# A graph network on one core: the sort's mask transfers issued from GpSimd, three GpSimd steps moved to VectorE and ScalarE, and the sort written ahead of the next pair's neighbours

## The chip, the core and the metric

The kernel runs on one core of one Trainium2 chip. A core has TensorE (PE, matrix products), VectorE (DVE), ScalarE (ACT), GpSimd (POOL) and SyncE (SP), each with its own instruction queue, executed in order, and 16 DMA engines that all queues share. PEld is PE's loading of weights. SP, ACT and POOL can issue DMAs. The time is the device time of one execution in microseconds (us): 5809.48 us is the median of three runs (5806.7 to 5821.54).

## The reference

The input is 16 graphs of 1024 nodes with 64 features `x`, a symmetric adjacency matrix `adj` (zeros and ones, ones on the diagonal) and a node mask. Four layers follow one another, each adding its result to `x`, and each starting from `h = max(layernorm(x), 0)`.

Layer 0 first thins the graph. Of each node with more than ten neighbours, every `skip`-th neighbour is removed, in both directions. Then, for each node and feature, three quantiles over the remaining neighbours are taken and mixed:

```python
skip = jnp.where(nb > T, (nb + K - 1) // K, 1)
rem = neigh & (sk > 1) & (rank % sk == sk - 1) & mask[:, :, None]
rem = rem | jnp.swapaxes(rem, 1, 2)
adj_d = jnp.where(rem, 0.0, adj_)
...
s = jnp.sort(vals, axis=2)        # the neighbours' values of each feature
for tau, w in zip((0.25, 0.5, 0.75), (0.25, 0.5, 0.25)):
    agg = agg + w * (v_lo + frac * (v_hi - v_lo))
```

A small two-layer network follows. Layer 1 is a gated recurrent update with messages summed through `adj`, layer 2 a small network on sums through `adj`, and layer 3 an attention whose scores come from `adj` and the features, with a softmax over the first node index.

## The kernel before

The kernel works on pairs of graphs, eight in all. Instead of sorting the neighbours of every node, it sorts all 1024 nodes once per feature and finds each quantile by counting.

- **`sort_begin`, `sort_pair` (L752 to L881)**: the sort of one pair, with the 128 combinations of graph and feature on the 128 partitions and the 1024 nodes along the row. A bitonic network of 55 steps runs on DVE. Each forward step writes a mask of which elements were swapped (L791 or L793), their maxima (L794) and minima (L795). Four steps make a group; the group's masks, 512 KB, lie in one of two buffers `swapped` and are stored to DRAM (`m_d`, L808). After the last step the kernel walks back through the network: it loads the groups in reverse (L821) and carries rank codes to the places that the elements came from (L826 to L839). L842 to L870 build tables of the sorted values, and L873 to L881 transpose the codes and store them (`y_d`).
- **`neighbours` (L884 to L983)**: for each graph, eight tiles of `adj` are loaded (`a`, L898), turned into zeros and ones (L899), cleared on the diagonal (L900, on POOL), and summed along the row (L904). PE transposes each tile (L910), ACT copies it out (L912) and stores it (`a_d`, L913) for layers 1 to 3. Four tiles form a half; then small steps (L919 to L929) give each node's step, ACT marks the removed neighbours (L933 to L935), PE combines the marks of both directions (L954) and ACT writes the thinned matrix `ndT` (L960). The buffers `ni`, `rem` and `cum` exist once.
- **`weights`, `select` (L986 to L1247)**: comparisons of rank codes (L1000, on DVE), then counting by matrix products and picking of the quantiles.
- **`compact`, `extras` (L1252 to L1399)**: nodes that fall outside the tables' range are collected and treated apart. A gather issued by POOL (L1296) fetches their rows.
- **`layers` (L1415 to L1622)**: the rest of layer 0 and layers 1 to 3 of one graph. Every pass over `adj` loads eight tiles (`adj_block`, L1495). L1521 copies the mask and L1530 two halves of `hT`, both on POOL.

The loop over pairs (L1656) runs, for pair `pr`: weights, selection and compaction of both graphs; extras; layers of both graphs; and then, for the next pair, `prepare` (the neighbours of its two graphs) and `sort_pair`; at the end `sort_begin` for the pair after that. All of this is written as straight code. A scheduler arranges it: among the instructions that are ready on an engine in its model of time, the one that was written first goes first. So the place in the program is a priority, and each queue's order, SP's and POOL's among them, is fixed when the kernel is built. The first pair's sort is marked as high priority and stands in front of its neighbours. The pool that holds the neighbours' working tiles (`ni`, `rem`, `cum`, `a`) is closed before the one with the next pair's weights is opened, so the weights can be given the same memory, and then wait for the neighbours' last reads.

The order in question:

```python
if pr + 1 < pairs:
    made = prepare(pr + 1, nb, nbp)
    sort_pair(pr + 1, cur, sop)
```

Of the kernel before, what the change touches and what calls it, by code (L numbers as in the profile page):

```python
# [42 lines left out]
def gnn_stack(ctx, tc, x, adj, nodemask, w, out):  # L43
# [736 lines left out]
    def sort_pair(pr, cur, sop):  # L780

        nxt = row4()
        groups = range(0, len(steps), GROUP)
        for k0 in groups:
            swapped = next(swaps)
            for k, (size, j) in enumerate(steps[k0 : k0 + GROUP]):
                of = cut(size, j)
                lo, hi = halves(cur, size, j, of)
                to_lo, to_hi = halves(nxt, size, j, of)
                if size == N:  # L790
                    nc.vector.tensor_tensor(side(swapped[:, k, :], size, j), *halves(cur, size, j)[::-1], op=ALU.is_gt)  # L791
                else:
                    nc.vector.tensor_tensor(side(swapped[:, k, :], size, j, of), hi, lo, op=ALU.is_gt)  # L793
                nc.vector.tensor_tensor(to_lo, lo, hi, op=ALU.max)  # L794
                nc.vector.tensor_tensor(to_hi, lo, hi, op=ALU.min)  # L795
                if odd_even(size, j):
                    ends_ = slice(None, None, size // j - 1)
                    nc.vector.tensor_copy(inner(nxt, size, j)[:, :, ends_], inner(cur, size, j)[:, :, ends_])
                cur, nxt = nxt, cur
                if size < N and size in CUT and j == 2 * CUT[size][2]:  # L800
                    rest_ = so.tile([P, 1], F32, name="rest_", bufs=2)
                    nc.vector.tensor_reduce(
                        rest_, cur.rearrange("p (x w) -> p x w", w=CUT[size][0])[..., CUT[size][1] :],
                        axis=AX.XY, op=ALU.max,
                    )
                    nc.vector.tensor_max(past, past, rest_)
            n = len(steps[k0 : k0 + GROUP])
            nc.sync.dma_start(m_d[k0 // GROUP, :, :n], swapped[:, :n])  # L808
        srt = row4()
        for g in range(8):  # L810
            nc.scalar.copy(
                srt.rearrange("p (b a g l) -> p g l a b", a=2, b=2, g=8)[:, g],
                cur.rearrange("p (l r a b) -> p r l a b", r=8, a=2, b=2)[:, 4 * (g & 1) + (g & 2) + (g >> 2)],
            )
        code = so.tile([P, N], U16, name="code")
        nc.sync.dma_start(code, c0_d)
        xo = so.tile([P, N // 2], U16, name="xo")
        for k0 in reversed(groups):
            swapped = next(swaps)
            n = len(steps[k0 : k0 + GROUP])  # L820
            nc.sync.dma_start(swapped[:, :n], m_d[k0 // GROUP, :, :n])  # L821
            for k, (size, j) in reversed(list(enumerate(steps[k0 : k0 + GROUP]))):
                of = cut(size, j) if size < N else None
                lo, hi = halves(code, size, j, of)
                d = side(xo, size, j, of)
                nc.vector.tensor_tensor(d, lo, hi, op=ALU.bitwise_xor)  # L826
                if of is None and not odd_even(size, j):
                    nc.vector.tensor_mul(xo, xo, swapped[:, k, :])
                else:
                    nc.vector.tensor_mul(d, d, side(swapped[:, k, :], size, j, of))  # L830
                if odd_even(size, j):
                    pairs_ = between(code, d, size, j)
                else:
                    pairs_ = None if j == size // 2 and size > 32 else both_sides(code, xo, j, of)
                if pairs_ is None:
                    nc.vector.tensor_tensor(lo, lo, d, op=ALU.bitwise_xor)
                    nc.vector.tensor_tensor(hi, hi, d, op=ALU.bitwise_xor)
                else:
                    nc.vector.tensor_tensor(pairs_[0], *pairs_, op=ALU.bitwise_xor)  # L839


        nc.vector.tensor_max(past, past, srt[:, 2 * WL * (NH - 1) : 2 * WL * (NH - 1) + 1])  # L842
        used = 2 * WL * NH

        def differences(step):
            fl = row4()[:, :used]
            nc.scalar.mul(fl[:, :step], srt[:, :step], SCALE)
            nc.vector.tensor_sub(fl[:, step:], srt[:, step:used], srt[:, : used - step])
            nc.scalar.mul(fl[:, step:], fl[:, step:], SCALE)
            return fl  # L850

        def parts(to, src):
            nc.scalar.copy(to[0], src)
            nc.vector.tensor_sub(to[1], src, to[0])

        dif = differences(2 * WL).rearrange("p (a b c) -> p a b c", b=2, c=WL)
        parts([ttab[:, :, k, :, :WL] for k in range(2)], dif)
        nc.sync.dma_start(t_d[pr * P : (pr + 1) * P], ttab.rearrange("p a b c d -> p a (b c d)"))
        dif = differences(WL).rearrange("p (w c) -> p w c", c=WL)
        ends = so.tile([P, WL], F32, name="ends")  # L860
        at = 0
        for k in STATS:
            w0, w1 = WIN[k]
            n = w1 - w0
            parts([wtab[:, at + 1 : at + n, e, :WL] for e in range(2)], dif[:, w0 + 1 : w1])
            nc.vector.tensor_add(ends, srt[:, WL * w0 : WL * (w0 + 1)], srt[:, WL * (w1 - 1) : WL * w1])
            nc.vector.tensor_scalar_mul(ends, ends, SCALE)
            parts([wtab[:, at, e, :WL] for e in range(2)], ends)
            at += n
        nc.sync.dma_start(w_d[pr * P : (pr + 1) * P], wtab.rearrange("p w a l -> p w (a l)"))  # L870

        cf = row4()
        nc.scalar.mul(cf, code, -4.0)  # L873
        cn = row4().bitcast(F16)[:, :N].rearrange("p (t k) -> p t k", k=P)
        for q in range(0, NT, 4):
            pc = sop.tile([P, 4, P], F32, name="ps")
            for t in range(4):
                nc.tensor.transpose(pc[:, t, :], cf[:, (q + t) * P : (q + t + 1) * P], ident)
            nc.scalar.copy(cn[:, q : q + 4, :], pc)
        for b in range(2):  # L880
            nc.sync.dma_start(y_d[pr * 2 + b], cn[:, :, b * C : (b + 1) * C])  # L881


    def neighbours(b, ndT, row10, qb, qz, nb, nbp):  # L884
# [9 lines left out]
        for t0 in range(0, NT, HT):  # L894
            cum = nb.tile([P, HT, N], F16, name="cum")
            for t in range(t0, t0 + HT):
                a = nb.tile([P, N], F32, name="a", bufs=2)
                nc.sync.dma_start(a, adj[b, t * P : (t + 1) * P, :])  # L898
                nc.vector.tensor_single_scalar(ni[:, t, :], a, 0.0, op=ALU.is_gt, saturate=False)  # L899
                nc.gpsimd.tensor_mul(  # L900
                    ni[:, t, t * P : (t + 1) * P], ni[:, t, t * P : (t + 1) * P], offdiag, saturate=False
                )

                nc.vector.tensor_tensor_scan(  # L904
                    cum[:, t - t0, :], ni[:, t, :], wide[:, t, pad - 1 : pad - 1 + N], 0.0, op0=ALU.add, op1=ALU.add
                )
                for q in range(0, NT, 4):
                    pt = nbp.tile([P, 4, P], F32, name="pk")
                    for k in range(4):
                        nc.tensor.transpose(pt[:, k, :], a[:, (q + k) * P : (q + k + 1) * P], ident)  # L910
                    at = nb.tile([P, 4, P], F32, name="at", bufs=3)
                    nc.scalar.copy(at, pt)  # L912
                    nc.scalar.dma_start(  # L913
                        a_d[b % 4, q : q + 4, :, t * P : (t + 1) * P].rearrange("j p n -> p j n"), at
                    )
# [499 lines left out]
    def layers(b, side_, agg, front, ly, lb, h0, xb, held=None):  # L1415
# [24 lines left out]
        def own(v):  # L1440
            return v.rearrange("p (t f) c -> p t f c", f=2)
# [76 lines left out]
            )  # L1518
        x1 = nd("xs", 2)
        mask = ly.tile([P, NT, 1], F32, name="mask")  # L1520
        nc.gpsimd.tensor_copy(own(mask), by_half(maskf[:, b * NT : (b + 1) * NT].rearrange("p (t o) -> p t o", o=1)))  # L1521
        nc.vector.tensor_mul(x1, by_node(py), mask.to_broadcast([P, NT, C]))
        nc.vector.tensor_add(x1, x1, xb)

# [2 lines left out]
        hT = transposed(h1, "hT")  # L1527
        both_ = ly.tile([P, 2, HALF], F32, name="two")
        for f in range(2):
            nc.gpsimd.tensor_copy(both_[f * C : (f + 1) * C, f, :], hT[f * C : (f + 1) * C])  # L1530
        mT = packed("mT")
        nc.scalar.activation(mT, dense_p([(l1w1_d, hT)]), AF.Relu, bias=l1b1_t, scale=1.0)
        m2 = big()
# [122 lines left out]
    for pr in range(pairs):  # L1656
# [18 lines left out]
        with ExitStack() as beside:  # L1675
# [14 lines left out]
            with (  # L1690
# [9 lines left out]
                for i, (ly, lb) in enumerate(((ly0, lb0), (ly1, lb1))):  # L1700
                    layers(pr * 2 + i, (pr * 2 + i) % 4, aggs[i], ly0, ly, lb, *heads[i], held[i])
                if pr + 1 < pairs:
                    made = prepare(pr + 1, nb, nbp)
                    sort_pair(pr + 1, cur, sop)
                if pr + 2 < pairs:
                    cur = sort_begin(pr + 2, sop)
    lasting.close()
# [46 lines left out]
```

## Time and profile before

| what | value |
|---|---|
| median of three runs | 5809.48 us (5806.7 to 5821.54) |
| profiled execution | 5811.5 us, span 5809.6 us |
| PE busy | 4320.3 us (74%) |
| DVE busy | 5034.4 us (87%) |
| ACT busy | 3811.5 us (66%) |
| POOL busy | 257.3 us (4%), 308 instructions |
| DMA moved | 551.49 MB, mean 95 GB/s |
| mask stores and loads of the sort (L808, L821) | 112 each, issued by SP |
| L900 on POOL | 128 instructions, 89.6 us |
| L1530 on POOL | 32 instructions, 24.4 us |
| L1521 on POOL | 16 instructions, 3.1 us |

A row of the profile names an engine, a source line, an operation and the tiles that it writes and reads (written, arrow, read), with its count and times. "Idle before" is the time that the engine stood still just before such an instruction, and the releaser is what ended it. The chain of waits follows the work that ended last back through whatever released it. A queue's name with a small q (SPq, POOLq) means the instruction queue of that engine, which issues DMAs. The granted clock is TensorE's, as a share of full speed. Busy shares are means over stages with different limits, so most of what follows is read from a single stage.

### The profile page before, as it was taken

How to read it: one execution, taken by the hardware profiler on the slowest of the kernel's cores; microseconds unless marked ns; L12 is line 12 of the kernel's file. 1: busy time of each engine (PE TensorE's matmuls, PEld its weight loads, DVE VectorE, ACT ScalarE, POOL GpSimd, SP SyncE). 2: the span in 40 equal slices, each digit the busy share in tenths (PEclk: the TensorE clock that was granted, in tenths of full speed). 3: DMA queues.
4: the chain of work that ended last, by engine and by line, in shares of the span. 5: the costliest groups of instructions: out<-in, count | busy, mean ns of one | idle time of the engine just before them, and what ended most of it. 6: DMA issues, size and time to landing. Idle time of an engine off the chain costs nothing.

```text
span 5809.6 us, 114773 instructions
## 1 busy us (share of the span) xinstructions
PE 4320.3 (74%) x45010; PEld 2712.1 (47%) x45010; DVE 5034.4 (87%) x13519; ACT 3811.5 (66%) x5753; POOL 257.3 (4%) x308
## 2 busy tenths in 40 slices
PE   1488686896768958788677886688866887768966
PEld 1355443554435544455434554355543554435542
DVE  9999878998799987998889988899888998887765
ACT  1586657775676856768567675766657866568735
POOL 3000000000000000000100001000000000000000
PEclk5699787997889968899788997889977998889977
DMA  4401363014621046210571105611255112630030
GB/s 129 126 28 40 97 228 103 26 37 125 222 80 35 28 136 221 73 32 27 161 228 45 40 30 176 210 37 37 64 190 169 33 40 83 214 115 9 19 100 5
DMA packets 523657, 551.49 MB, mean 95 GB/s; under 512 B 264065, under 2 KB 413825, under 8 KB 523105
## 3 DMA queue, kind: packets, MB, share of 16 engines
q1 hardware_dynamic: 380704, 459.65, 25.3%
q10 hardware_dynamic: 140064, 81.84, 4.6%
q8 instruction: 355, 5.82, 0.4%
q0 software_dynamic: 2336, 2.57, 0.2%
q14 instruction: 198, 1.61, 0.1%
HBM read 360.17 MB, written 183.76 MB: 94 GB/s over the span
## 4 chain that ended last, share of the span: by engine, by line
DVE 37%; PE 32%; ACT 16%; DMA 11%; issue 3%; POOL 0%; SPq 0%; ACTq 0%; DVEq 0%; POOLq 0%
PE comb L1122 10%; ACT sign L1177 5%; DVE y L1193 5%; PE cand L1222 4%; PE comb L1311 4%; DVE cand L1230 3%; PE bank L1502 3%; DMA a<-in_adj_dram 2%; DVE cum L904 2%; ACT y L1130 2%; DMA adjT<-a_d 2%; DVE wt L1000 2%; DMA a_d<-at 2%; PE pk L954 2%; DVE code L839 2%
## 5 line engine op out<-in xcount | busy, mean ns | idle before, releaser
L1122 PE MATMUL comb<-wt,ndT 128*128 128x512 fp8e5 x6144 | 1445.0, 388 | 143.3 <-ACT sign L1177 112.6
L1130 ACT ACTIVATE y<-comb,qb 128x512 int16<-128x512 f32 x1152 | 744.9, 710 | 526.1 <-PE comb L1122 526.1
L1122 PEld LDWEIGHTS <-ndT 128*128 128x128 fp8e5 x6144 | 592.5, 99 | 862.8 <-issue 235.1
L1177 ACT ACTIVATE sign<-comb,lower 128x1024 fp8e5<-128x1024 int16 (+1 forms) x640 | 694.6, 1085 | 0.0
L1177 ACT ACTIVATE sign<-comb,half 128x1024 fp8e5<-128x1024 int16 (+1 forms) x640 | 689.2, 1077 | 0.0
L1193 DVE TENSOR_TENSOR y<-y 128x512 uint16<-128x512 uint16 (+5 forms) x896 | 669.5, 788 | 10.8 <-PE comb L1175 10.0
L1222 PE MATMUL cand<-vtab,sign 128*128 128x48 f16 (+1 forms) x18432 | 661.4, 191 | 17.4 <-DVE agg L1099 10.1
L1222 PEld LDWEIGHTS <-sign 128*128 128x128 fp8e5 x18432 | 636.6, 96 | 76.9 <-issue 23.6
L1230 DVE COPY_PREDICATED cand<-w_f,cand 128x256 f32<-128x256 uint16 (+1 forms) x1536 | 529.1, 377 | 75.9 <-PE cand L1222 73.6
L1175 PE MATMUL comb<-ident_b,y 128*128 128x128 bf16 x4608 | 307.2, 218 | 102.9 <-ACT sign L1177 70.6
L954 PE MATMUL pk<-ident_b,ni 128*128 128x128 bf16 x1024 | 234.9, 251 | 160.2 <-ACT at L912 90.3
L1175 PEld LDWEIGHTS <-y 128*128 128x128 bf16 x4608 | 284.8, 97 | 128.1 <-issue 127.8
L954 PE MATMUL pk<-minus_b,rem 128*128 128x128 bf16 x1024 | 235.9, 256 | 145.2 <-ACT rem L935 145.2
L912 ACT COPY at<-pk 128x512 f32<-128x512 f32 x256 | 146.3, 583 | 287.8 <-PE pk L910 150.1
L1000 DVE TENSOR_SCALAR wt<-node 128x2048 uint8<-128x2048 f16 x224 | 261.6, 1219 | 53.1 <-PE comb L1311 52.6
L904 DVE TENSOR_TENSOR_SCAN cum<-ni 128x1024 f16<-128x1024 fp8e5 x128 | 292.7, 2291 | 16.4 <-POOL ni L900 16.4
L910 PE MATMUL pk<-ident,a 128*128 128x128 f32 x1024 | 186.2, 325 | 134.1 <-DMA a<-in_adj_dram 90.8
L1502 PE MATMUL bank<-adjT,nd 128*64 128x512 f32 x896 | 252.1, 631 | 32.2 <-DMA adjT<-a_d 31.9
L794 DVE TENSOR_TENSOR s<-s 128x384 f32<-128x384 f32 (+4 forms) x440 | 264.9, 602 | 0.0
L1188 DVE TENSOR_SCALAR y<-y 128x4608 int16<-128x4608 int16 x128 | 173.4, 1354 | 104.1 <-ACT y L1130 104.1
L795 DVE TENSOR_TENSOR s<-s 128x384 f32<-128x384 f32 (+4 forms) x440 | 262.9, 597 | 0.0
L1502 PE MATMUL bank<-att,hs 128*64 128x512 f32 x512 | 192.7, 868 | 79.3 <-ACT hs L1612 78.6
(382 smaller groups left out, 8383.2 us busy)
## 6 DMA issues: line engine op xcount, KB each, us to landing
adjT<-a_d SPq DMA_DIRECT2D x336, 512.0 KB
a<-in_adj_dram SPq DMA_DIRECT2D x128, 512.0 KB
a_d<-at ACTq DMA_DIRECT2D x256, 256.0 KB
m_d<-swapped SPq DMA_DIRECT2D x104, 512.0 KB
swapped<-m_d SPq DMA_DIRECT2D x104, 512.0 KB
n_d<-nat SPq DMA_DIRECT2D x128, 128.0 KB
x_d<-xr SPq DMA_DIRECT2D x112, 128.0 KB
comb_x<-x_d ACTq DMA_DIRECT2D x24, 512.0 KB
```

Of the source, the lines that this page charges most:

```text
L794: nc.vector.tensor_tensor(to_lo, lo, hi, op=ALU.max)
L904: nc.vector.tensor_tensor_scan(cum[:, t - t0, :], ni[:, t, :], wide[:, t, pad - 1 : pad - 1 + N], 0.0, op0=ALU.add, op1=ALU.add)
L954: nc.tensor.matmul(pk[:, n % 4, :], lhs, rhs, start=(n % 4 == 0 and m == 0), stop=(m == len(terms) - 1 and last),)
L1000: nc.vector.tensor_scalar(wt[g][:, :, k : k + 4, :].bitcast(U8), node, 4.0 * (25 + CODE * (8 * g + k)), 4.0 * 26, op0=ALU.add, op1=ALU.min,)
L1122: nc.tensor.matmul(pw, ndT[:, j, t * P : (t + 1) * P], wt[1 + g8][:, j].rearrange("p w c -> p (w c)"), start=(j == 0), stop=(j == NT - 1),)
L1130: nc.scalar.activation(y[:, 0, chunks, at : at + 8 * d_].rearrange("p q (w d) -> p q w d", d=d_), pw.rearrange("p (w q d) -> p q w d", w=8 ...
L1175: nc.tensor.transpose(pt[:, q - q0, :], y[:, 0, q, :].bitcast(BF16), ident_b)
L1177: nc.scalar.activation(signs[tl][s][:, q0:q1, :], pt.bitcast(I16), AF.Sign, bias=before[s], scale=-1.0, saturate=False,)
L1193: nc.vector.tensor_tensor(v[:, :, :, :n], v[:, :, :, :n], v[:, :, :, n : 2 * n], op=ALU.max)
L1222: nc.tensor.matmul(cand[:, e, at : at + 12 * d_].rearrange("p (d l) -> p d l", l=12), signs[tl][sec][:, chunk, :], tab[:, q, :, half_ * 12 ...
L1230: nc.vector.copy_predicated(v[:, :, :, dst : dst + k], mk.to_broadcast([P, 2, C // 2, k]), v[:, :, :, frm : frm + k])
L1502: nc.tensor.matmul(po[to : to + C, :], lhs, rhs[:, f * HALF : (f + 1) * HALF], start=(j == 0), stop=(j == NT - 1))
```

## The change

The masks of the sort are stored and loaded through POOL's queue instead of SP's. Three elementwise steps leave POOL: the clearing of the diagonal and the copy of the mask go to DVE, the copy of `hT` goes to ACT. POOL keeps the memsets (L746, L891, L1334), a small copy (L968), the gather (L1296) and the loading of constants. In the loop, `sort_pair` for the next pair is written ahead of `prepare`, so it takes precedence over the neighbours wherever both are ready.

```diff
-            nc.sync.dma_start(m_d[k0 // GROUP, :, :n], swapped[:, :n])
+            nc.gpsimd.dma_start(m_d[k0 // GROUP, :, :n], swapped[:, :n])
...
-            nc.sync.dma_start(swapped[:, :n], m_d[k0 // GROUP, :, :n])
+            nc.gpsimd.dma_start(swapped[:, :n], m_d[k0 // GROUP, :, :n])
...
-                nc.gpsimd.tensor_mul(
+                nc.vector.tensor_mul(
                     ni[:, t, t * P : (t + 1) * P], ni[:, t, t * P : (t + 1) * P], offdiag, saturate=False
                 )
...
-        nc.gpsimd.tensor_copy(own(mask), by_half(maskf[:, b * NT : (b + 1) * NT].rearrange("p (t o) -> p t o", o=1)))
+        nc.vector.tensor_copy(own(mask), by_half(maskf[:, b * NT : (b + 1) * NT].rearrange("p (t o) -> p t o", o=1)))
...
-            nc.gpsimd.tensor_copy(both_[f * C : (f + 1) * C, f, :], hT[f * C : (f + 1) * C])
+            nc.scalar.copy(both_[f * C : (f + 1) * C, f, :], hT[f * C : (f + 1) * C])
...
                 if pr + 1 < pairs:
+                    sort_pair(pr + 1, cur, sop)
                     made = prepare(pr + 1, nb, nbp)
-                    sort_pair(pr + 1, cur, sop)
```

## The prediction

> **What bounds the kernel now.** The page comes first: which engine is full, and what the chain of waits that ended last is made of.
>
> ```profile
> PE 4320.3 (74%) x45010; PEld 2712.1 (47%) x45010; DVE 5034.4 (87%) x13519; ACT 3811.5 (66%) x5753; POOL 257.3 (4%) x308
> DVE 37%; PE 32%; ACT 16%; DMA 11%; issue 3%; POOL 0%; SPq 0%; ACTq 0%; DVEq 0%; POOLq 0%
> ```
>
> DVE is the fullest engine, but 13% of it is idle, and the chain changes engine often. The order of the starts shows a period: the weights (L1000) of pairs 1 to 7 begin at about 973, 1679, 2389, 3093, 3795, 4499 and 5199 us, every 700 to 710 us. A period is some 370 us of selection and compaction, and a side stage of about 316 us in which extras, layers, the next pair's neighbours and the next pair's sort share the engines. Next the busy time of each engine in stretches of one side stage (1365 to 1681):
>
> ```profile
> 1474.00:1510.00 36.00, 33.76 (x284) 20.50 (x284) 31.88 (x100) 17.66 (x32) 4.52 (x7) 0.95 0.61 213
> 1510.00:1556.00 46.00, 37.27 (x154) 15.64 (x155) 25.74 (x81) 25.70 (x37) 1.97 (x4) 0.96 0.89 310
> 1556.00:1653.00 97.00, 64.34 (x298) 29.11 (x296) 89.67 (x244) 74.95 (x100) 1.18 (x2) 0.77 0.54 163
> 1653.00:1669.00 16.00, 8.10 (x156) 6.79 (x152) 15.18 (x49) 9.18 (x15) 0.00 (x0) 0.90 0.41 99
> 1669.00:1681.00 12.00, 2.34 (x9) 1.57 (x10) 5.90 (x37) 3.64 (x6) 0.00 (x0) 0.50 0.22 33
> ```
>
> The columns are PE, PEld, DVE, ACT, POOL, clock, DMA share, GB/s. DVE is idle for 20.3 of 46 us from 1510 to 1556, and the last 12 us are nearly empty on every engine. SP's queue says why the sort stops in the first hole:
>
> ```profile
> 1533.46 14.07 SPq L1495 DMA_DIRECT2D adjT<-a_d  x8
> 1547.62 0.44 SPq L898 DMA_DIRECT2D a<-in_adj_dram  x1
> 1548.10 0.90 SPq L821 DMA_DIRECT2D swapped<-m_d  x2
> ```
>
> Two loads of the sort's masks leave back to back at 1548.10, though DVE had used up both buffers by 1509: they stood behind adjacency loads that wait for PE. The same hole is in every side stage. The chain shows the second hole:
>
> ```profile
> 1548.10 7.78 DMA swapped<-m_d
> ...
> 1668.00 0.64 DVE code L839
> 1668.66 1.07 ACT s L873
> ...
> 1673.32 2.93 DMA y_d<-s
> 1676.31 2.68 DMA node<-y_d
> 1680.98 13.73 DVE wt L1000 x12
> ```
>
> The sort's last step ends at 1668.6; its result crosses ACT, PE and DRAM twice before the weights start 12.3 us later. The neighbours' last large ACT step ends beside it, and layers ended at 1653:
>
> ```profile
> 1662.22 0.99 ACT L960 ACTIVATE ndT<-pk 128x512 fp8e5<-128x512 f32 x2 [0.25 <-PE pk L954]
> ```
>
> **The change part by part.** The profiled execution took 5811.5 us (span 5809.6, 1.9 around it), 2.0 above the median shown, 5809.48; the sum is made against it.
>
> *Mask transfers (L808, L821) from SP to POOL.* 112 stores and 112 loads, 28 per sort. SP's issue takes 0.32 us. POOL's plain DMAs at the start take 0.48 to 1.09 each and land after 1.5 to 3.0 us, but they are small (at most 32 KB); the sort's loads land in 3.97 and 7.78 us on the chain. So POOL adds between 0.16 and 0.77 us to a load. A group of four backward steps is about 4 x (0.42 + 0.42 + 0.69) = 6.1 us of DVE and the loads are one group ahead, which covers it; uncovered, 112 x 0.77 = 86 us is the upper end. I take 0.
> The Trainium skill, "SBUF — State Buffer", section "SBUF: two separate sides", speaks against this: descriptors of a GpSimd DMA cannot be written while DVE runs a two-port instruction, and a DMA of 620 ns took 3100. By that page an estimate would be 112 x 2.5 = 280 us if all loads lay open; no run here shows it, and the sort's own steps have two inputs, which the page excepts from that trap.
> What does SP gain? The hole, 20.3 us of idle DVE per side stage, is open to the sort. It isn't free: that stretch moves 310 GB/s at a DMA share of 0.89, and four loads more (2.1 MB) take 6.8 us of it. [...]
> New order on POOL: a store waits for DVE's compares (on SP the longest such wait is 16.1 us), and behind it stand the row gather (L1296), for which PE waits, the memsets (L891, L1334) and L968. A gather held for 16 us in all 16 batches would cost 256 us. I take 0: its index also comes from DVE, and later in DVE's order than a store put ahead of it.
>
> *Sort traced ahead of neighbours.* The sort then wins DVE whenever both are ready. Of its backward steps 45 us (L826, L828, L830, L836, L837, L839) lie after 1556; the hole has room for 20, and the scans and tests of the neighbours (L904, L899), 24 us of DVE from 1400 to 1556, now give way. So it should end between 1560 and 1600 instead of 1669, and its 12.3 us tail comes under other work. The end passes to the neighbours. They are four halves in a row (one buffer of L904's scans), each DVE, then ACT and PE: first scans at 1369, 1430, 1494, 1563. The best guide is the first stage, where the sort already has high priority: there halves start at 53, 115, 174 and 207 and end by 252, 199 us against 294 here, though the ten small steps of one half (L919 to L929) took from 80 to 102 between sort steps. So layers and loads, more than the sort, set the pace of the neighbours. If they still end at 1663, the weights follow 4.7 us later (from the issue of node's load to L1000), at 1668: 13 us saved. If they end with layers at 1653, 23 are saved, and 26 if node is loaded ahead: the upper end. If they slip by 13, nothing is saved; by 26, as much as the spread small steps held one half up in the first stage (its scans end at 78, its next ACT step starts at 103), 13 are lost: the lower end. I take a slip of 5, nearer to none, because their second and third halves lie under the sort and the last one doesn't: 8 us saved, 7 x 8 = -56.
>
> *L900 to DVE.* 128 products of 128x128; nearest rows 0.18 (L1201, 128x64), 0.22 (L1369, 128x128 uint16) and 0.29 (L1553, f32). 128 x 0.22 = 28 us, less the 16.4 that L904 waited for POOL: +12, of which some 10 where DVE is full. Ends: 0 and +21.
> *L1521 to DVE*: 16 x 0.16 = 2.6 us, early in a batch's layers while PE works: 0, or +3 uncovered.
> *L1530 to ACT*: 32 copies; nearest row 0.58 (L1315, 64x512): 19 us. They stand between hT and mT on ACT, where PE's product takes 1.06 us: 2 x 0.58 - 1.06 = 0.1 per batch, +2; +19 if another order leaves them open.
>
> *What POOL stops doing.*
>
> ```profile
> L900 POOL TENSOR_TENSOR ni<-ni,offdiag x128: 406/647/2326, 51.7 to 5129.5; 128x128 fp8e5<-128x128 fp8e5 x128
> L1296 POOL DMA_INDIRECT rows<-n_d,who x16: 952/1026/6518, 446.2 to 5549.1; - x16
> ```
>
> The first gather of pairs 1 to 7 takes 6.5 us and lands after 8.9; the second takes 0.97. Before the slow ones POOL ran products and copies, before the fast ones one small copy. If the mixture is the reason, 7 x 4 = 28 us go; but pair 0's first gather, behind products alone, took 1.3. Between 0 and -28 I take -14.
>
> Sum: -56 + 10 + 2 - 14, and +2 for the first stage, where 16 products less POOL's waits meet a full DVE: -56. 5811.5 - 56 = 5755.5, or 5754 on the scale of the median.
>
> **The rivals.** *Slower: the neighbours become the tail.* For it: with the sort first, ACT is idle early and the neighbours' ACT work (L933 to L960) falls into 1556 to 1653, where ACT is busy for 75 of 97 us with layers ahead of it. Against: the first stage's pace. It decides from a slip of 13 us on; with 26, the -56 turns into 7 x 13 = +91: 5754 + 56 + 91 = 5901.
> *Everything is gained*: SP also serves adjacency loads sooner, layers lose a competitor on DVE after 1556, and the neighbours end with layers. 7 x 24 (between 23 and 26) = 168 instead of 56, and the whole 28 of the gather: 5754 - 112 - 14 = 5628. Against: layers already come first.
> *No effect*: the sort was hidden, the neighbours slip by 11 to 13 us, and 0 to 14 us are left, the gather's -14 and the small costs of +14 cancel: 5796 to 5810, and DVE's new idle time stands at the end of the side stage.
> *POOL's queue is slow*: loads late by 0.77 us and the 6.8 us of shared DMA on the path in seven stages: 5754 + 86 + 48 = 5888. Against: loads are a group ahead.
>
> **How the numbers follow.** The likeliest has 0.47 (its own range 5690 to 5790), everything gained 0.12, no effect 0.09, neighbours as tail 0.24, slow queue 0.08. About 0.3%, 17 us, is what a measurement of this kernel can tell from no change; so faster 0.59, same 0.09, slower 0.32. The range, 5635 to 5890, holds all but 'everything gained' and the far end of 'the neighbours as tail'.
>
> **What would show it.** Right: no hole in DVE after the first third of layers; mask loads leave POOL right after the step that frees their buffer; the sort's last step well before layers end; the weights following the neighbours' last ACT step by 5 us; a period of about 695 to 700. Wrong: DVE waiting for masks, PE for the gather; L960 running 15 us or more past layers; the first gather still at 6.5 us. What would upset it all is a different order of layers or selection, since every order here follows from the trace order.

## The result, and the profile after

The changed kernel takes 6102.52 us (median of four runs, 6100.36 to 6124.92) beside 5810.12 us for the kernel before on the same chip: a ratio of 1.0502, 95% interval 1.0486 to 1.0518. The forecast was 5754. The profiled execution took 6101.26 us, with a span of 6099.5 and a granted clock of 0.815 (0.850 before). The lower clock goes with the order (0.826 with the order alone changed, 0.852 with the old order put back, both below), and the layers end no later at it: 671 us after the weights on average over five periods, 677 before.

The page of the changed kernel, its first line and its chain of waits:

```profile
PE 4416.2 (72%) x45010; PEld 2788.8 (46%) x45010; DVE 5090.4 (83%) x13663; ACT 3821.9 (63%) x5783; POOL 231.9 (4%) x356
DVE 37%; PE 35%; ACT 15%; DMA 8%; issue 3%; SPq 1%; ACTq 0%; DVEq 0%; POOLq 0%
```

DVE has 56 us more to do, of which L900 accounts for 128 x 0.28 = 36 us, and yet its share fell from 87% to 83%: the 290 us more are waiting, not work. The weights (L1000) of pairs 0 to 7 start at 275, 1030, 1775, 2522, 3267, 4014, 4762 and 5488 us. By the same count the kernel before has them at 275, 975, 1681, 2391, 3095, 3797, 4501 and 5200. The period is 745 to 748 us where it was 702 to 710, the first is 755 instead of 700, the last 726 instead of 699, and the seven differences add up to 288 us, so all of the loss lies in the seven side stages.

The same side stage as in the prediction (the period that starts at 1030), as busy time of each engine in five stretches of the changed kernel; columns as before, PE, PEld, DVE, ACT, POOL, clock, DMA share, GB/s:

```profile
1437.00:1497.00 60.00, 19.79 (x388) 18.36 (x387) 58.70 (x186) 15.38 (x15) 1.61 (x3) 0.50 0.26 84
1505.00:1560.00 55.00, 43.98 (x182) 24.37 (x183) 43.27 (x128) 28.59 (x41) 2.69 (x5) 0.66 0.60 198
1560.00:1616.00 56.00, 44.39 (x185) 18.87 (x186) 46.47 (x156) 26.38 (x42) 1.07 (x2) 0.88 0.77 262
1616.00:1701.00 85.00, 58.01 (x383) 28.33 (x382) 63.00 (x191) 70.23 (x97) 0.69 (x1) 0.80 0.52 152
1701.00:1775.00 74.00, 29.76 (x299) 23.96 (x297) 70.00 (x150) 41.28 (x56) 3.75 (x7) 0.65 0.38 127
```

Two things are new. In the first 60 us DVE is full while PE and ACT have little to do. And the last 74 us, after the layers have ended at about 1701, have no counterpart before, where layers ended 28 us ahead of the weights. VectorE is not idle there: of its 70 us, 54 are forward steps (L793 to L802) of the sort of the pair after next, of which 30 of 55 have run by the next weights and none had before. They are written later than the neighbours and fill what these leave.

The first stretch, in VectorE's own order (start, duration, line, tiles):

```profile
1435.45 0.68 DVE L899 TENSOR_SCALAR ni<-a 128x1024 fp8e5<-128x1024 f32 x1
...
1436.66 0.28 DVE L900 TENSOR_TENSOR ni<-ni,offdiag 128x128 fp8e5<-128x128 fp8e5 x1
1436.86 1.08 DVE L1362 TENSOR_SCALAR y_x<-y_x 128x3584 int16<-128x3584 int16 x1
...
1496.83 2.28 DVE L904 TENSOR_TENSOR_SCAN cum<-ni 128x1024 f16<-128x1024 fp8e5 x1
...
1501.23 0.16 DVE L919 TENSOR_TENSOR sk<-cum,ni 128x4 f32<-128x4 f16 x1
```

The fourth tile of the neighbours' first half is ready for its scan at 1436.9 and is scanned 60 us later. Adding up the instructions in between by line, 60 are the sort's (some 22 us) and 125 belong to the extras (some 37 us). Before, this half's last scan and its ten small steps ran at 1391.9 to 1396.2, just ahead of the extras' first DVE instruction at 1398.9. With the sort in front, the half misses that place, and then falls behind the extras too, which were written earlier still. ScalarE gets its work only now:

```profile
1508.23 1.15 ACT L933 ACTIVATE sq<-cum,sk 128x1024 f32<-128x1024 f16 x1 [25.29 <-DVE sk L927]
```

The halves form a chain: one `cum` buffer, and `ni` and `rem` are shared by the two graphs. Counted from the start of the weights, the small steps of the four halves stand at 470, 559, 676 and 711 us (period of 1775) against 420, 477, 568 and 640 before (period of 1681), so they are late by 50, 82, 108 and 71 us. The second graph can be seen to wait for the first: the memset of its `ni` (L891) stands at 647 us (period of 1030), where PE's last products on the first graph's `ni` (L954) end, and both stood at 516 to 517 before. The neighbours' last large ACT step (L960) ends on average at 737 instead of 687 over five periods, and layers at 671 instead of 677. So the neighbours end 66 us past the layers, 10 before.

The sort itself ended early, as forecast. Its last step, from DVE's order and from ACT's:

```profile
1611.57 0.69 DVE L839 TENSOR_TENSOR code<-code,xo 128x1024 uint16<-128x1024 uint16 x1
```

```profile
1615.87 1.04 ACT L873 ACTIVATE s<-code 128x1024 f32<-128x1024 uint16 x1
```

That is 582 us after the weights, where it was 694. But nothing waits for it there. The chain of waits into the next weights runs through the neighbours, up to their last steps on VectorE (L971 to L983), between which early steps of the sort of the pair after next stand:

```profile
1761.15 3.63 PE pk L954 x35
1764.80 0.61 ACT ndT L960
...
1765.45 1.75 PE pk L964 x64
1767.22 0.17 DVE last L971
1767.39 0.60 DVE swapped L793
...
1774.11 0.60 DVE node L995 x3
...
1776.24 12.58 DVE wt L1000 x11
```

Those early steps make up 27 of the last 73 us of the chain. Whether they delay the neighbours was not tested. From its small steps to its last L960 the last half takes 25 us here (period of 1030) and took 51 before; but in the last of the seven side stages, where there is no pair after next, the period grew by only 27 us, and by 37 to 45 in the five before it. So up to some 14 us of each stage may be due to them or to what else is begun for that pair.

The mask loads leave POOL as soon as the step that frees their buffer is done, and POOL's issue takes 0.54 us at the median (0.74 at most):

```profile
1454.22 0.54 POOL L821 DMA_DIRECT2D swapped<-m_d  x1 [17.92 <-DVE xo L828]
```

### The profile page after: what moved, and what is told of

Same layout as the page of the kernel before. It is cut to its first block, busy times and chain, and to the rows that moved or that the text cites. A ratio compares the mean times of both kernels' runs of the same rounds, so it can differ in the third digit from the quotient of the medians.

```text
span 6099.5 us, 114699 instructions
## 1 busy us (share of the span) xinstructions
PE 4416.2 (72%) x45010; PEld 2788.8 (46%) x45010; DVE 5090.4 (83%) x13663; ACT 3821.9 (63%) x5783; POOL 231.9 (4%) x356
## 4 chain that ended last, share of the span: by engine, by line
DVE 37%; PE 35%; ACT 15%; DMA 8%; issue 3%; SPq 1%; ACTq 0%; DVEq 0%; POOLq 0%
PE comb L1122 10%; DVE y L1193 6%; PE cand L1222 5%; PE bank L1502 4%; PE comb L1311 4%; DMA adjT<-a_d 3%; DMA a<-in_adj_dram 3%; ACT sign L1177 3%; DVE cand L1230 2%; ACT y L1130 2%; DVE cum L904 2%; DVE wt L1000 2%; PE pk L954 2%; DVE y_x L1033 1%; DVE y L1188 1%
## 5 line engine op out<-in xcount | busy, mean ns | idle before, releaser
L1222 PEld LDWEIGHTS <-sign 128*128 128x128 fp8e5 x18432 | 630.0, 96 | 88.9 <-issue 35.9
L954 PE MATMUL pk<-minus_b,rem 128*128 128x128 bf16 x1024 | 260.5, 274 | 275.1 <-ACT rem L935 275.1
L1188 DVE TENSOR_SCALAR y<-y 128x4608 int16<-128x4608 int16 x128 | 173.5, 1356 | 249.3 <-ACT y L1130 249.2
L954 PE MATMUL pk<-ident_b,ni 128*128 128x128 bf16 x1024 | 257.2, 268 | 135.4 <-ACT ndT L960 107.7
L933 ACT ACTIVATE sq<-cum,sk 128x1024 f32<-128x1024 f16 x128 | 146.9, 1148 | 297.3 <-DVE sk L927 295.4
L954 PEld LDWEIGHTS <-rem 128*128 128x128 fp8e5 x1024 | 126.3, 123 | 426.8 <-ACT rem L935 335.7
L1385 PE MATMUL cand<-tab,sign_x 112*64 112x96 f16 x3072 | 135.1, 279 | 235.0 <-DVE agg_x L1097 160.5
L910 PEld LDWEIGHTS pk<-ident,a 128*128 128x128 f32 x1024 | 141.7, 172 | 345.0 <-issue 212.4
```

The lines of the kernel that those rows point to most:

```text
L954: nc.tensor.matmul(pk[:, n % 4, :], lhs, rhs, start=(n % 4 == 0 and m == 0), stop=(m == len(terms) - 1 and last),)
L1222: nc.tensor.matmul(cand[:, e, at : at + 12 * d_].rearrange("p (d l) -> p d l", l=12), signs[tl][sec][:, chunk, :], tab[:, q, :, half_ * 12 ...
```

## The experiments

The theory was called 'order': the sort, written ahead, takes VectorE's slots from the neighbours, and these become the tail. Its rivals: 'queue' (masks on POOL, or the memset of `ni`, which waits in POOL's queue for some 88 us in each side stage, delay the neighbours) and 'element work' (the products of L900 on VectorE lie in the neighbours' chain). Each median (of four runs; five of sort_between, two of small_first and scans_first) is compared with that of the kernel before on the same chip (5818 to 5825 us).

| run | what differs | us | ratio to before, 95% interval |
|---|---|---|---|
| order_only | before, with the sort written first | 6112.60 | 1.0494 (1.0475 to 1.0513) |
| old_order | changed kernel, neighbours written first | 5760.38 | 0.9894 (0.9878 to 0.9911) |
| queue_only | before, with the masks on POOL's queue | 5698.86 | 0.9803 (0.9774 to 0.9831) |
| elements_only | before, with the element work moved | 5783.29 | 0.9934 (0.9917 to 0.9950) |
| small_first | changed kernel, small steps ahead of the sort | 6077.54 | 1.0420 (1.0388 to 1.0453) |
| scans_first | changed kernel, scans ahead of the sort | 5931.58 | 1.0170 (1.0141 to 1.0200) |
| both_first | changed kernel, both ahead | 5797.05 | 0.9956 (0.9906 to 1.0006) |
| sort_between | changed kernel, sort between the two graphs | 5802.95 | 0.9964 (0.9943 to 0.9985) |
| queue_products | queue_only and L900 on VectorE | 5727.78 | 0.9839 (0.9813 to 0.9864) |
| queue_act | queue_only and L1530 on ScalarE | 5735.38 | 0.9870 (0.9845 to 0.9895) |
| loads_only | before, with the mask loads on POOL | 5780.12 | 0.9933 (0.9912 to 0.9955) |
| stores_only | before, with the mask stores on POOL | 5753.29 | 0.9889 (0.9859 to 0.9919) |

### The change, part by part

**The order alone.**

```diff
-                    made = prepare(pr + 1, nb, nbp)
                     sort_pair(pr + 1, cur, sop)
+                    made = prepare(pr + 1, nb, nbp)
```

> The kernel before with one edit: the sort is traced ahead of the next pair's neighbours; masks stay on SP, the element work stays on GpSimd. Theory 'order' (the sort, ahead of the neighbours, takes VectorE from their scans and small steps, ScalarE runs dry in the first part of the side stage, and the neighbours end some 70 us past the layers in seven stages): nearly all of the +292 us is here, 6040 to 6150 us, period about 740 to 750. Theory 'queue' (the masks and the memsets that wait in GpSimd's queue cost the time): the order alone costs little or gains, 5740 to 5830. Theory 'element work' (the products on VectorE, 128 x 0.28 us = 36 us in the neighbours' chain of scans): 5740 to 5830 as well.

Measured +295 us: the whole loss, without any mask on POOL and without a product on VectorE. The period is 743 to 752 us and the halves' small steps stand at 467, 577, 671 and 708 (period of 1777), nearly as in the changed kernel. This is about what 'order' expected.

**The changed kernel in the old order.**

```diff
-                    sort_pair(pr + 1, cur, sop)
                     made = prepare(pr + 1, nb, nbp)
+                    sort_pair(pr + 1, cur, sop)
```

> The changed kernel with the old order put back: masks on GpSimd's queue and the element work moved, neighbours traced ahead of the sort. Theory 'order': the loss is gone, and the hole of 20 us of idle VectorE in seven side stages may be filled: 5670 to 5830 us. Theory 'queue': 6000 or more. Theory 'element work': 5850 to 6100.

Measured -57 us. The loss is gone, so 'queue' and 'element work' are out as its cause. It also happens to be the size that I had forecast for the whole change (-56), for another reason.

**The masks' move alone.**

```diff
-            nc.sync.dma_start(m_d[k0 // GROUP, :, :n], swapped[:, :n])
+            nc.gpsimd.dma_start(m_d[k0 // GROUP, :, :n], swapped[:, :n])
...
-            nc.sync.dma_start(swapped[:, :n], m_d[k0 // GROUP, :, :n])
+            nc.gpsimd.dma_start(swapped[:, :n], m_d[k0 // GROUP, :, :n])
```

> The kernel before with the mask stores and loads alone moved from SP to GpSimd's queue; element work stays on GpSimd. My prediction's step: nothing is paid for a load on the other queue, and the hole in VectorE closes, so between 5670 (7 x 20 us gained) and 5815. Theory 'queue': 5900 or more, with VectorE waiting for masks. Theory 'order': within 5670 to 5830; it says nothing finer.

Measured -119 us, the fastest kernel of all, ahead of the kernel before and of the changed one: 5698.86 us, 2.0% under the kernel before (1.7 to 2.3%). Its busy line, and the stretch of its side stage that answers to the hole (537 to 583 us after the weights, as 1510 to 1556 was before):

```profile
PE 4281.6 (75%) x45010; PEld 2706.7 (48%) x45010; DVE 5018.1 (88%) x13519; ACT 3780.0 (66%) x5739; POOL 403.1 (7%) x532
```

```profile
1491.00:1537.00 46.00, 40.35 (x196) 17.58 (x191) 42.33 (x123) 29.42 (x44) 3.58 (x6) 0.93 0.91 315
```

DVE is busy for 42.3 of 46 us where it was 25.7, at the same DMA share (0.91 to 0.89) and nearly the same rate (315 to 310 GB/s): the transfers of the masks were taken in beside the rest. The sort's last step now stands at 660 us after the weights, the neighbours' last ACT step ends at 676 (their last step on VectorE at 682), layers end at 687 to 688, and the next weights start at 686.

**The element work alone.**

```diff
-                nc.gpsimd.tensor_mul(
+                nc.vector.tensor_mul(
...
-        nc.gpsimd.tensor_copy(own(mask), by_half(...))
+        nc.vector.tensor_copy(own(mask), by_half(...))
...
-            nc.gpsimd.tensor_copy(both_[...], hT[...])
+            nc.scalar.copy(both_[...], hT[...])
```

> The kernel before with the three element moves alone (the products with offdiag and the mask's copy to VectorE, the two half copies to ScalarE). My prediction's terms: +12 for these, -14 for the gather, so 5800 to 5825, and the first gather of pairs 1 to 7 at 1 us instead of 6.5 if the mixture on GpSimd was its reason. Theory 'element work': 5850 to 6100. Theory 'order': under 5850.

Measured -34 us: I had costed it at nothing, and 5783 lies under the 5800 to 5825 that I expected. VectorE is busy for 37.9 of 46 us in the stretch that starts 537 us after the weights, though the masks stay on SP:

```profile
1502.00:1548.00 46.00, 35.49 (x222) 16.58 (x221) 37.85 (x131) 22.80 (x37) 0.69 (x1) 0.96 0.91 307
```

The first gather of pairs 1 to 6 did not get faster (6.46 to 6.48 us), though POOL now has no product and no large copy:

```profile
L1296 POOL DMA_INDIRECT rows<-n_d,who x16: 945/1014/6477, 447.1 to 5519.3; - x16
```

So the mixture of work on POOL is not the reason for the slow gather. In order_only, whose POOL still has that mixture, the gather is fast:

```profile
L1296 POOL DMA_INDIRECT rows<-n_d,who x16: 954/1030/1325, 447.5 to 5844.6; - x16
```

### Which part of the neighbours the sort held up

The scheduler's priority can be raised for a few instructions. All four runs start from the changed kernel. In the first three, the sort stays ahead of the rest of the neighbours; the raised steps go ahead of the extras and the layers too, not of the sort alone. Pairs are counted from 0, and pair 0 is not touched.

**The ten small steps ahead of the sort.**

```diff
+            with tc.high_priority() if b >= 2 else ExitStack():
-            nc.vector.tensor_tensor(sk[:, 2, :], cum[:, :, N - 1], ni[:, t0 : t0 + HT, N - 1], op=ALU.add)
+                nc.vector.tensor_tensor(sk[:, 2, :], cum[:, :, N - 1], ni[:, t0 : t0 + HT, N - 1], op=ALU.add)
...
```

> The changed kernel with the ten small steps of each half of the neighbours (sk, nbi) of pairs 1 to 7 put ahead of the sort again in the planner's priorities; the scans and tests stay behind the sort. Theory 'small steps' (what my prediction used for its slower rival: the spread small steps hold a half up): at least half of the +292 us comes back, 5950 or less. Theory 'scans' (the fourth scan of the first half stands 62 us behind the sort's steps on VectorE, from the adjacency tile's test at 1435 to the scan at 1497, and the small steps follow it within 9 us): little comes back, 6040 to 6110. Theory 'ScalarE and TensorE' (the later trace order hurts the neighbours on ACT and PE, not on VectorE): 6040 or more.

Measured 1.0420 where the changed kernel has 1.0502, 0.8% of some 5820 us or about 48 us back. The first half's small steps stay at 468 to 475 us after the weights, since the fourth scan, on which they depend, has not moved. So 'small steps' is out; the other two theories both allow this time.

**The test, the product and the scan ahead of the sort.**

```diff
+                with tc.high_priority() if b >= 2 else ExitStack():
-                nc.vector.tensor_single_scalar(ni[:, t, :], a, 0.0, op=ALU.is_gt, saturate=False)
+                    nc.vector.tensor_single_scalar(ni[:, t, :], a, 0.0, op=ALU.is_gt, saturate=False)
...
```

> The changed kernel with the test, the product and the scan (L899 to L904) of pairs 1 to 7 put ahead of the sort in the planner's priorities; the small steps stay behind it. Theory 'scans': most comes back, 5760 to 5950. Theory 'small steps': 6000 or more. Theory 'ScalarE and TensorE': 6040 or more.

Measured 1.0170, about 193 us back, as 'scans' expected. The first half is on time again (small steps at 411), the last one is not (675).

**Both.**

```diff
+                with tc.high_priority() if b >= 2 else ExitStack():
-                nc.vector.tensor_single_scalar(ni[:, t, :], a, 0.0, op=ALU.is_gt, saturate=False)
+                    nc.vector.tensor_single_scalar(ni[:, t, :], a, 0.0, op=ALU.is_gt, saturate=False)
...
+            with tc.high_priority() if b >= 2 else ExitStack():
-            nc.vector.tensor_tensor(sk[:, 2, :], cum[:, :, N - 1], ni[:, t0 : t0 + HT, N - 1], op=ALU.add)
+                nc.vector.tensor_tensor(sk[:, 2, :], cum[:, :, N - 1], ni[:, t0 : t0 + HT, N - 1], op=ALU.add)
...
```

> The changed kernel with all VectorE work of the neighbours (test, product, scan, small steps) of pairs 1 to 7 ahead of the sort; only their ScalarE, TensorE and DMA work still stands behind it. Theories 'scans' and 'small steps': about the time of the old order, 5730 to 5830. Theory 'ScalarE and TensorE': 6000 or more.

Measured 0.9956, all of the loss against the kernel before is back (old_order stands at 0.9894). ACT's total wait for the small steps, from its waits in the changed kernel and in this one (total, times, longest):

```profile
ACT sq L933 <- DVE sk L927: 295.4, 25, 30.7
```

```profile
ACT sq L933 <- DVE sk L927: 86.0, 13, 30.4
```

So the loss is made on VectorE: the neighbours' PE, ACT and DMA work still stands behind the sort here, and no loss is left. The small steps are worth some 48 us by themselves, and another 125 (1.0170 to 0.9956) once the scans are on time: a half is only as early as the later of the two. The tail has changed sides again. The neighbours' last ACT step ends at 675 us, the sort's last step stands at 680 to 684, and the layers, which now give way to the neighbours on VectorE, end at 705 to 709, some 3 us past the start of the next weights.

**The sort between the two graphs.**

```diff
             neighbours(pr * 2 + i, *made[i], nb, nbp)
+            if between is not None and i == 0:
+                between()
...
-                    sort_pair(pr + 1, cur, sop)
-                    made = prepare(pr + 1, nb, nbp)
+                    made = prepare(pr + 1, nb, nbp, lambda: sort_pair(pr + 1, cur, sop))
```

> The changed kernel with the sort traced between the two graphs' neighbours of the next pair. Theory 'scans': the first graph is not held up (its halves' small steps at about 415 and 475 us after the weights instead of 470 and 560), the second graph starts on time, and its later half starts when the sort is nearly done, so 5750 to 5900. Theory 'ScalarE and TensorE': the loss is halved at best, 5900 to 6000.

Measured 0.9964. The first graph's small steps stand at 406 and 467 us, as in the old order (412 and 473); the last half is late by some 25 us (658 against 631 in old_order), and the neighbours' last ACT step ends at 691 to 698 us with the layers done at 671 to 680. This is what 'scans' expected: the loss follows the place of the sort half by half.

A second buffer for `ni`, which would let the second graph start before the first has ended, was not tried.

### Why masks alone gain twice what masks and element work gain

**Masks, and the products on VectorE**: queue_only, with

```diff
-                nc.gpsimd.tensor_mul(
+                nc.vector.tensor_mul(
```

> Masks on GpSimd's queue, order as before, and of the element work the products with offdiag (L900) alone on VectorE. Theory 'full VectorE': once the hole is filled, VectorE has no slack left in the side stage, so the 128 x 0.283 us = 36 us of products come on top of 5699: 5720 to 5750, about half or more of the 61 us by which masks and element work together (5760) stand over masks alone. Rival 'queue': the products on VectorE are free as they were without the masks' move (element work alone gained 34 us), and the 61 us are from the copies on ScalarE: 5670 to 5705.

**Masks, and the copies of `hT` on ScalarE**: queue_only, with

```diff
-            nc.gpsimd.tensor_copy(both_[f * C : (f + 1) * C, f, :], hT[f * C : (f + 1) * C])
+            nc.scalar.copy(both_[f * C : (f + 1) * C, f, :], hT[f * C : (f + 1) * C])
```

> Masks on GpSimd's queue, order as before, and of the element work the two half copies (L1530) alone on ScalarE. Theory 'full VectorE': 0 to +20 us over 5699 (32 x 0.61 us on ScalarE, mostly beside TensorE). Rival 'copies': +30 to +60, 5730 to 5760.

Measured +29 and +37 us over queue_only, and the two together (65) make up the 61 us between queue_only and old_order (the first is near the limit of the measurement, its interval overlaps queue_only's). So 'full VectorE' accounts for the products, and for the copies its rival was right: with the copies on ACT the layers end at 694 to 695 us after the weights instead of 687, while the neighbours' last step on VectorE stays at 682. In queue_only layers and neighbours end within a few us of each other, so a delay of either one can become the new tail.

**The mask loads alone.**

```diff
-            nc.sync.dma_start(swapped[:, :n], m_d[k0 // GROUP, :, :n])
+            nc.gpsimd.dma_start(swapped[:, :n], m_d[k0 // GROUP, :, :n])
```

> The kernel before with the mask loads alone on GpSimd's queue; the stores stay on SP. Theory 'hole' (the gain of the masks' move is that loads no longer stand behind SP's adjacency loads): most of the 119 us are there, 5690 to 5740, and VectorE is busy for 40 of the 46 us in which it was busy for 26. Rival 'stores' (SP's own queue is what gained, since a store that waits for VectorE's compares held up the loads behind it for up to 17 us): 5760 or more.

**The mask stores alone.**

```diff
-            nc.sync.dma_start(m_d[k0 // GROUP, :, :n], swapped[:, :n])
+            nc.gpsimd.dma_start(m_d[k0 // GROUP, :, :n], swapped[:, :n])
```

> The kernel before with the mask stores alone on GpSimd's queue; the loads stay on SP. The loads alone gained about 39 us and both together 119, so if the two parts simply add, the stores alone give 80 us, 5740. Theory 'hole': the hole of 20 us of idle VectorE stays, as the loads still stand behind SP's adjacency loads, so at most 30 us are gained, 5790 to 5820, and the two parts need each other. Rival 'SP's order': the stores alone move the adjacency loads of the second graph ahead on SP (15th and 16th at 583 and 585 us after the weights with both moved, 617 and 632 before), 5730 to 5770.

Measured -39 and -69 us; together -108, nearly the -119 of both. The stretch of the hole, in loads_only and in stores_only:

```profile
1503.00:1549.00 46.00, 35.01 (x142) 14.14 (x141) 38.70 (x133) 22.55 (x34) 5.27 (x7) 0.91 0.92 324
```

```profile
1503.00:1549.00 46.00, 38.21 (x187) 17.25 (x183) 35.88 (x125) 30.16 (x44) 0.83 (x2) 0.93 0.77 266
```

The loads alone fill the hole (38.7 of 46 us) and bring the sort's last step from 698 to 670 us, and still gain only a third, so 'hole' is out as the main source, and the rivals' times hold in both runs. In stores_only, whose loads stay on SP, VectorE is busy for 35.9 of the 46 us as well. What the stores add can be read on SP: the last adjacency load of the next pair's neighbours. Before, in the period that starts at 975, and in queue_only, in the period of 954:

```profile
1602.84 0.33 SPq L898 DMA_DIRECT2D a<-in_adj_dram  x1
```

```profile
1538.61 0.34 SPq L898 DMA_DIRECT2D a<-in_adj_dram  x1
```

That is 628 and 585 us after the weights. In loads_only it is 619, in stores_only 583 (periods of 1671 and 1659). Without the stores in its order, SP reaches the second graph's adjacency tiles some 45 us sooner, and the neighbours end earlier. Whether this comes from the order that the scheduler then gives SP or from a store that waits at SP's head was not separated.

## Why the prediction was wrong

- **The bound.** In the main the views were read rightly: one side stage per period, a hole that stands in SP's queue, a tail of two chains (sort, neighbours) close together. Two readings were off: the slow gathers are those of six pairs, 1 to 6 (pair 7's took 1.07 us), and the longest wait of a store on SP was 21.8 us, not 16.1.
- **Masks to POOL, taken at 0.** Right for the cost: VectorE waits for mask loads for 3.9 us in all, 7.2 before. What it gains was put down to the sort in the new order alone, and sized too small: 119 us in the old order, with the stores giving the larger part.
- **Sort ahead of neighbours, taken at -56.** Here the prediction failed. The parts about the sort held: its last step at 582 us after the weights (forecast between 585 and 625), the hole halved or better (VectorE busy for 43.3 of 55 and 46.5 of 56 us), its tail of 12 us covered. The step that failed is "I take a slip of 5, nearer to none": the neighbours slipped by 50 (737 against 687). It rested on "layers and loads, more than the sort, set the pace of the neighbours"; the runs showed that the place of their scans and small steps on VectorE sets it (both_first takes the loss back, order_only makes all of it). By the prediction's own sum, 7 x (50 - 13) = +259 in place of -56, that is 5811.5 + 259 = 6071 us for the profiled execution, which took 6101. The rest is in the first period, which grew by 56 us and not by 37, in the next five, by some 41 each, and in the last, by only 27.
- **Why the slip was wrong.** The comparison was the first stage, where the sort also has priority and the neighbours still ran well. But there VectorE has next to nothing besides the two (some 7 us of 210). In the side stage a half that misses its place also falls behind the extras: of the 60 us that the first half lost, the sort's own steps were 22 and the extras' 37. Then the delay grew to 82 and 108 us in the second and third half; the single buffers between them are the reason as read from the program and from the memset at 647 us, not tested alone. The sum of the sort's work that overtakes was never the price of being overtaken.
- **The rival "the neighbours become the tail"** had the mechanism, the place and the point from which it decides (13 us), and was given 0.24 and a slip of 26, taken from the same first stage. Its 5901 us was 200 short.
- **L900, L1521 and L1530, taken at +12, and at +2 for the first stage.** In the kernel before, the three moves gain 34 us, and why was not isolated; in its trace the hole is mostly filled and the sort's last step stands some 5 us earlier on average over the seven side stages. On top of the masks' move they cost 61. A price for such a move holds only for one state of the schedule: after the masks' move, L900's 36 us cost some 29, and the copies that I hid behind PE's product cost 37.
- **The gather, taken at -14.** It did become fast in the changed kernel (PE's wait for its rows fell from 101.1 to 67.7 us in all), but with the order and not with the mixture on POOL (order_only has it fast with that mixture); it is as slow as before in old_order, elements_only and queue_only.

## What to carry to other kernels

When one chain is put ahead of another on a shared engine, do not price the other's delay by the work that overtakes it. Find the gap in which the overtaken step ran, ask what stands next in that queue with a higher priority, and follow the delay through every single buffer behind it. A change of several parts should be tried part by part: here one part cost 5% and hid another that gains 2%.

## What the runs showed of the hardware

**DMAs issued by GpSimd beside a busy VectorE.** The Trainium skill, "SBUF — State Buffer", section "SBUF: two separate sides", says that GpSimd cannot write a DMA's descriptors while VectorE runs an instruction that takes both ports. In old_order a mask store took 1.70 us to issue instead of the usual 0.54 while VectorE ran a test of 1.35 us (POOL's order, then VectorE's):

```profile
1699.59 1.70 POOL L808 DMA_DIRECT2D m_d<-swapped  x1 [88.45 <-DVE swapped L793]
```

```profile
1699.82 1.35 DVE L1188 TENSOR_SCALAR y<-y 128x4608 int16<-128x4608 int16 x1
```

The direction agrees with the page. In the eleven kernels with masks on POOL, 97 transfers took over 0.7 us to issue, and every one of them ended 0.116 to 0.124 us after the end of a VectorE step with one input (L899, L1047, L1188 or L1362 of the kernel before). The size is small here: four of 112 stores of old_order took about 1.70 us, and four of its 112 loads 1.06 to 1.44 us; all 112 stores together took 68 us of POOL's time, 8 more than 112 x 0.54, and VectorE waited 8.8 us in all for mask loads. In the changed kernel no load took more than 0.74 us, and the 43 that were issued beside the sort's own steps alone, which have two inputs, took at most 0.54 us. The 280 us that an estimate by that page gave do not occur.

**The slow gather is still open.** In the kernel before and in queue_only the first gather of each of pairs 1 to 6 starts beside VectorE instructions that follow one another without a gap for 5.6 us, and ends 0.9 us after the last of them. That looks like the same exclusion. In the changed kernel and in order_only no sort step stands there, VectorE has gaps of 35 ns, and the gather takes 1.05 to 1.08 us. But in sort_between VectorE runs without a gap for the same 5.6 us, and the gather takes 1.02 us. No run separates the cause.
